# Two graph attention layers in one kernel: where the gather of a layer 0 unit's own rows stands on GpSimd's queue

## The chip, the cores and the metric

The kernel runs on one core of one Trainium2 chip. The metric is the device time of one launch in microseconds. Engines are named as in the profile: PE (TensorE, with PEld for its weight loads), DVE (VectorE), ACT (ScalarE), POOL (GpSimd) and SP (SyncE). POOL and SP issue most of the DMAs; a queue's name with a q (SPq) is its issuing side.

## What is computed

`x` holds 8 graphs of 2048 nodes with 256 channels, `adj` one symmetric adjacency matrix for all of them, in which a node has some 9 neighbours on average. Both layers attend over neighbours, add the input back and normalise:

```python
# layer 0: x = layernorm(x + gnn0(x))
h1, h2, h3 = inp @ W1, inp @ W2, inp @ W3
e = leaky_relu(einsum('bnd,bmd->bnm', h1, h2), 0.2)
e = where(adj > 0, e, -1e12)
h = relu(softmax(e, -1) @ h3)
# layer 1: x = layernorm(x + gnn1(x)), 4 heads of 64
q = (h @ W).reshape(B, N, 4, 64)
e = leaky_relu(e_src[:, :, None] + e_dst[:, None], 0.2)   # q . a_src, q . a_dst
attn = softmax(where(adj > 0, e, -9e15), axis=2)
h = elu(einsum('bijh,bjhd->bihd', attn, q))
```

## The kernel before, in words

**Tiling.** The nodes are sorted by degree and cut into 16 tiles of 128 (`order[:, t]` holds the node numbers of tile `t`). `SLOTS` gives each tile the number K of neighbour slots that its largest node needs: 12 for the sparsest tile to 36 for the densest. A unit is one tile of one half of the batch (4 graphs) in one layer, so there are 64 units: `units` lists 32 of layer 0 (half 0, then half 1, each from the sparsest tile to the densest), then 32 of layer 1. For each slot k of a unit, an indirect DMA on POOL gathers, for 128 nodes, the row of their k-th neighbour: 4 graphs x 256 channels in float32, 4 KB for a node, 512 KB in all. Layer 0 gathers from `xg[h]`, a copy of `x` with the 4 graphs of half h side by side, layer 1 from `qg[h]`.

**A layer 0 unit** goes through four generators.
- `before0` (L525 to L544) gathers the unit's own 128 rows into `xo` (L526, L527; the helper's DMA is L196), and has SP copy them, rearranged, to `xr` for the residual (L531, four DMAs). After four ticks PE transposes `xo` (`transposed`, L417; ACT copies the result, L419), and `projected` (L427) multiplies it by W1 W2^T to give `g`.
- `logits0` multiplies the gathered rows by `g` on DVE (L562: 4 instructions a slot, one a graph) and takes the softmax over the K slots.
- `sums0` makes diagonal matrices of the weights on ACT (`dg`, L659) and adds the weighted rows on PE (L639, 16 matmuls a slot).
- `after0` transposes the sums, multiplies by W3, adds `xr` (L699 on DVE), takes the statistics (L384) and normalises (L395 to L407 on ACT and DVE), writes the rows (L714), and projects them for layer 1 (L723); POOL scatters that to `qg` (L204).

**The ring.** Gathered rows go into a ring of 16 buffers of 2 slots each (`CHUNK`); `chunk_job` issues a chunk's two gathers. A buffer comes free when PE has summed its second slot, so POOL waits at a gather for that matmul. In the first half of layer 0, the ring also takes the adjacency rows (`nb`, L196) from which `neighbours` makes each tile's list on DVE (L505 to L519).

**The order of the work.** The program is written out as a simulation: `tick` (L955) lets `pump` issue all chunk gathers for which there are credits, advances the logits by up to two slots, and each of the queues `starts`, `ends` and `lists` by up to two steps. The main loop (L972) runs through the units; each slot of `sums` is a tick. When half of unit j's slots are summed (L990), `before` of unit j + 3 is put on `starts`, so its first step, with the gather of `xo`, is issued in the next ticks. `before` of the first three units is queued at the start. As unit j = 2 to 9 opens, POOL also issues a part of the copy `xg[1]` (L984), which marks those openings in the trace. POOL's instructions keep exactly the order in which the program issues them; those of the other engines are ordered by the scheduler of the framework, which goes by the program's order and by when it takes their inputs to be ready. Every engine then works through its list in order.

**Buffers.** `xown` has two buffers for `xo`; one comes free when PE's transposes and SP's four copies have read it. `xres` has three for `xr`; one comes free when L699 of its unit has read it, and SP waits for that at L531.

Of the kernel before, what the change touches and what calls it, by code (L numbers as in the profile page):

```python
# [11 lines left out]
F32 = mybir.dt.float32  # L12
# [10 lines left out]
P = 128  # L23
# [106 lines left out]
def fast_path(  # L130
# [26 lines left out]
    NT = N // P  # L157
    KC = C // P
    HB = B // 2
    HC = HB * C  # L160
# [9 lines left out]
    xop = ctx.enter_context(tc.tile_pool(name="xown", bufs=2))  # L170
# [20 lines left out]
    def wide_tile(name):  # L191
        return wp.tile([P, 2 * QW], F32, tag="t", name=name)

    def gather(dst, table, index):

        nc.gpsimd.indirect_dma_start(  # L196
            out=dst, out_offset=None, in_=table, in_offset=AT(ap=index, axis=0),
            bounds_check=table.shape[0] - 1, oob_is_err=False,
        )
# [12 lines left out]
    xg = [tc.dram_tile([N, HC], F32, name=f"xg_{h}") for h in range(2)]  # L212
# [102 lines left out]
    order = const.tile([P, NT], I32, tag="order", name="order")  # L315
# [32 lines left out]
    def checks():  # L348

        worst = wide_tile("worst")[:, :P]  # L350
        nc.gpsimd.memset(worst, 0.0)
        bad = const.tile([P, NT + 3], F32, tag="bad", name="bad")
        found, known = bad[:, NT + 1 : NT + 2], bad[:, NT + 2 : NT + 3]
        nc.vector.tensor_scalar(bad[:, :NT], degs, 0.5, None, ALU.is_lt)
        listless = wide_tile("listless")[:, :total]
        nc.vector.tensor_scalar(listless, neg, 0.0, 0.0, ALU.is_lt, ALU.add, accum_out=found)
        nc.vector.tensor_reduce(known, degs, AX.X, ALU.add)
        nc.vector.tensor_tensor(known, known, found, ALU.add)
        nc.vector.tensor_scalar(bad[:, NT : NT + 1], known, float(total), None, ALU.not_equal)
        nc.vector.tensor_reduce(worst[:, 0:1], bad[:, : NT + 1], AX.X, ALU.max)  # L360
        yield
        pb = ps_tile("ps_bad")
        nc.tensor.transpose(pb[:, :P], worst, ident)
        yield
        most = const.tile([P, 1], F32, tag="most", name="most")
        nc.vector.tensor_reduce(most[0:1, :], pb[0:1, :P], AX.X, ALU.max)
        nc.vector.tensor_copy(flag, most[0:1, :])
        yield
        nc.vector.scalar_tensor_tensor(half, half, 2.0 * N, orderR, ALU.mult, ALU.add)
        for h in range(2):  # L370
            for j in range(2):
                nc.vector.tensor_scalar(
                    oidx[:, h, j], half, float((h * HB + j) * N), None, ALU.add
                )
# [37 lines left out]
    def transposed(src, name, dst):  # L412

        for i in range(2):
            pt = ps_tile(f"ps_t_{name}_{i}")
            for j in range(4):
                nc.tensor.transpose(pt[:, ts(j, P)], src[:, ts(4 * i + j, P)], ident)  # L417
            yield
            nc.scalar.copy(dst[:, ts(i, 512)], pt)  # L419
        yield  # L420

    def projected(srcT, weight, name, evict):
        for i in range(2):
            pp = ps_tile(f"ps_p_{name}_{i}")
            for j in range(2):
                for k in range(KC):
                    nc.tensor.matmul(  # L427
                        pp[:, ts(j, C)],
                        lhsT=srcT[:, ts((2 * i + j) * KC + k, P)],
                        rhs=weight[:, k, :],  # L430
                        start=(k == 0),
                        stop=(k == KC - 1),
                    )
            yield
            evict(i, pp)
        yield

    class Unit:
        def __init__(self, layer, h, t):
            self.layer, self.h, self.t = layer, h, t  # L440
            self.K = SLOTS[t]
            self.name = f"{layer}_{h}_{t}"

            n = self.K if self.K <= RING * CHUNK * 3 // 4 else -(-self.K // 2)
            self.parts = [(k, min(n, self.K - k)) for k in range(0, self.K, n)]
            self.chunks = [[] for _ in self.parts]
            self.p = [None] * len(self.parts)
            self.ps = [None] * len(self.parts)

            self.m, self.s = [], []  # L450
            self.ready = False


# [39 lines left out]
    def neighbours(t):  # L493
        K, o = SLOTS[t], offs[t]
        while t not in loaded:
            yield
        v = loaded[t].bitcast(I16)[:, :N]
        if t in up[:3]:
            numbered(loaded[t])
            nc.vector.memset(loaded[t][:, N // 2 :], 0.0)  # L500


        some = sp.tile([P, 8 * BLOCKS], F32, tag="some", name=f"some_{t}", bufs=2)
        for i in range(BLOCKS):
            nc.vector.max(some[:, ts(i, 8)], v[:, N * i // BLOCKS : N * (i + 1) // BLOCKS])  # L505
            if i % 8 == 7:
                yield
        credits[0] += 1
        rounds = -(-K // 8)
        m = sp.tile([P, 40], F32, tag="m", name=f"m_{t}")  # L510
        for i in range(rounds):
            nc.vector.max(m[:, ts(i, 8)], some)
            if i + 1 < rounds:
                nc.vector.match_replace(some, m[:, ts(i, 8)], some, 0.0)
            yield
        nc.vector.tensor_scalar(neg[:, o : o + K], m[:, :K], 0.5, LOWEST, ALU.is_lt, ALU.mult)
        far = sp.tile([P, 40], F32, tag="far", name=f"far_{t}", bufs=2)[:, :K]
        nc.vector.tensor_scalar(far, m[:, :K], 0.5, FAR, ALU.is_lt, ALU.mult)
        nc.vector.scalar_tensor_tensor(  # L519
            idx[:, o : o + K], m[:, :K], 1.0, far, ALU.subtract, ALU.add  # L520
        )
        listed[t] = True


    def before0(u):  # L525
        xo = xop.tile([P, HC], F32, tag="xo", name=f"xo_{u.name}")  # L526
        gather(xo, xg[u.h][:, :], order[:, u.t : u.t + 1])  # L527
        u.xr = xrp.tile([P, 2, HW], F32, tag="xr", name=f"xr_{u.name}")
        for r in range(2):
            for c in range(2):  # L530
                nc.sync.dma_start(  # L531
                    u.xr[64 * c : 64 * c + 64, r, :], xo[64 * r : 64 * r + 64, ts(c, HW)]
                )
        for _ in range(4):
            yield
        xT = wide_tile(f"xT_{u.name}")
        yield from transposed(xo, f"x_{u.name}", xT)
        while scored[0] < u.index - 1:
            yield
        u.g = gp.tile([P, HC], F32, tag="g", name=f"g_{u.name}")  # L540
        yield from projected(
            xT, w.A, f"g_{u.name}", lambda i, pp: nc.scalar.copy(u.g[:, ts(i, 512)], pp)
        )
        u.ready = True  # L544
# [369 lines left out]
    units = [Unit(0, h, t) for h in range(2) for t in up]  # L914
# [19 lines left out]
    for j, u in enumerate(units):  # L934
        u.index = j
    before = (before0, before1)
    logits = (logits0, logits1)
    sums = (sums0, sums1)
# [8 lines left out]
    def finish(u):  # L947
        yield from after[u.layer](u)
# [6 lines left out]
    def tick(limit):  # L955
        pump()
        while late and late[0][0] <= clock[0]:
            late.popleft()[1]()
        for _ in range(2):
            if ahead[0] < limit:  # L960
                ahead[0] += next(stream, 0)
        for queue in queues:
            for _ in range(min(len(queue), 2)):
                if queue and next(queue[0], queue) is queue:
                    queue.popleft()
        clock[0] += 1
# [5 lines left out]
    for j, u in enumerate(units):  # L972
        begun = False
        if 0 < j and j + 2 < NT:
            lists.append(neighbours(up[j + 2]))
        if j == NT:
            ends.append(checks())
        while len(ends) > 1:
            tick(0)
        if 2 <= j < 10:  # L980
            b, i = divmod(j - 2, 2)
            n = ts(i, N // 2)

            nc.gpsimd.dma_start(xg[1][n, ts(b, C)], x[HB + b, n])  # L984
        left = float(u.K)
        for share in sums[u.layer](u):
            ahead[0] -= share
            left -= share
            tick(left + units[min(j + 1, len(units) - 1)].K + LEAD)
            if not begun and left <= u.K / 2 and j + 3 < len(units):  # L990
                begun = True
                v = units[j + 3]
                starts.append(before[v.layer](v))
        ends.append(finish(u))
# [300 lines left out]
```

## Time and profile before

| | us |
|---|---|
| median of 3 runs | 2709.94 (2703.99 to 2711.37) |
| the profiled execution's own time | 2598.36 |
| its span, first to last instruction | 2596.3 |
| busy: PE, DVE, ACT, POOL | 1816.4 (70%), 2148.3 (83%), 1441.4 (56%), 1532.3 (59%) |
| first and last gather of `xo` | 99.22 and 1417.09 |
| one gather of `xo` on POOL (median of 32) | 1.07 |
| mean granted TensorE clock | 0.85 |

Times in views of the trace are counted from the span's start. A line of the timeline has the start, the duration, the engine and the kernel's line, the operation, output and inputs, and in brackets how long the engine stood idle before it and what ended that. A line of the waits has who waited for what, the sum, the number of times and the longest. Layer 0 fills the profile from about 95 us to 1600 us and layer 1 the rest. The setup before it sorts the nodes.

### The profile page before, as it was taken

The numbers are of one execution on the slowest core, as the hardware profiler recorded it, in microseconds if no ns is written. First come the engines' busy times: TensorE is split into PE (matmuls) and PEld (weight loads), VectorE is DVE, ScalarE is ACT, GpSimd is POOL, SyncE is SP. The second block draws the span as 40 slices with busy tenths as digits, with TensorE's granted clock in tenths as the row PEclk, the third lists the DMA queues.
The fourth block names the chain that finished last, engine by engine and source line by source line (L and its number), as shares of the span: only waits on it lengthen the run. The fifth ranks groups of instructions, "written<-read, shape, count | busy, mean of one in ns | idle before, by whom it ended". The sixth has DMA issues, their size and how long they took to land. (4 is left out here: it accounts for less than half of the span.)

```text
span 2596.3 us, 52231 instructions
## 1 busy us (share of the span) xinstructions
PE 1816.4 (70%) x16675; PEld 989.4 (38%) x16675; DVE 2148.3 (83%) x7073; ACT 1441.4 (56%) x4849; POOL 1532.3 (59%) x1486
## 2 busy tenths in 40 slices
PE   1167797878778787788888878756475666764774
PEld 0145464545445455455555544212121222221221
DVE  6799899899889677777788885789888788988896
ACT  6245475656566556655666657454356556643455
POOL 3464455555555444535455555677677777776774
PEclk9588898989888788988898989878788788887877
DMA  9898787888875566767788768898799999987993
GB/s 382 276 338 273 257 313 267 302 285 280 269 270 194 186 218 240 247 231 235 255 264 284 257 206 273 301 342 327 273 341 355 349 339 367 349 320 270 325 358 106
DMA packets 249419, 734.92 MB, mean 283 GB/s; under 512 B 63200, under 2 KB 72544, under 8 KB 246704
## 3 DMA queue, kind: packets, MB, share of 16 engines
q0 software_dynamic: 192512, 645.89, 70.4%
q1 hardware_dynamic: 55360, 84.44, 9.6%
q8 instruction: 135, 2.21, 0.3%
q14 instruction: 148, 1.21, 0.1%
q10 hardware_dynamic: 1264, 1.18, 0.1%
HBM read 708.35 MB, written 76.09 MB: 302 GB/s over the span
## 5 line engine op out<-in xcount | busy, mean ns | idle before, releaser
L562 DVE CUSTOM_DVE_ANT_0 j<-s,g 128x256 bf16<-128x256 f32 x2384 | 1007.7, 423 | 197.7 <-DMA s<-xg,idx 127.2
L196 POOL DMA_INDIRECT s<-xg,idx x596 | 634.3, 1064 | 625.4 <-PE acc L639 413.5
L639 PE MATMUL acc<-s,ident 64*64 64x512 f32 x4768 | 610.9, 664 | 350.9 <-issue 296.7
L639 PE MATMUL acc<-s,dg 64*64 64x256 f32 x9536 | 706.1, 418 | 187.7 <-ACT dg L659 176.1
L196 POOL DMA_INDIRECT s<-qg,idx x596 | 606.7, 1018 | 242.0 <-issue 130.4
L659 ACT ACTIVATE dg<-twice,e 128x64 f32<-128x64 f32 x2384 | 617.6, 337 | 107.3 <-PE acc L639 101.8
L840 DVE TENSOR_TENSOR s<-s,p 128x2048 f32<-128x2048 f32 (+1 forms) x260 | 574.0, 2229 | 0.0
L639 PEld LDWEIGHTS acc<-s,dg 64*64 64x64 f32 x9536 | 383.1, 144 | 452.1 <-ACT dg L659 256.3
L639 PEld LDWEIGHTS acc<-s,ident 64*64 64x64 f32 x4768 | 210.4, 149 | 743.8 <-issue 600.0
L836 ACT ACTIVATE s<-s,e 128x64 f32<-128x64 f32 x1408 | 342.7, 335 | 47.7 <-DVE e L804 39.6
L395 ACT ACTIVATE z<-st,roots 128x4 f32<-128x4 f32 x64 | 19.1, 298 | 410.1 <-DVE st L384 410.1
L562 DVE DVE_READ_ACCUMULATOR2_ANT e<- 128x1 f32 x2384 | 194.0, 81 | 0.0
L204 POOL DMA_INDIRECT out_dram<-o,oidx x128 | 130.6, 1020 | 68.1 <-ACT o L407 32.2
L774 DVE TENSOR_TENSOR e<-s,own 128x32 f32<-128x32 f32 (+1 forms) x306 | 55.7, 186 | 121.5 <-DMA s<-qg,idx 120.3
L417 PE MATMUL ps_t_x<-ident,xo 128*128 128x128 f32 x256 | 55.4, 359 | 120.0 <-DMA xo<-xg,order 120.0
L723 PE MATMUL ps_q<-wqs,x1T 128*128 128x264 f32 x512 | 137.8, 407 | 2.1 <-ACT x1T L419 2.1
L427 PE MATMUL ps_p_h<-w_sb,hT 128*128 128x256 f32 x512 | 130.4, 399 | 5.6 <-ACT hT L419 5.6
L427 PE MATMUL ps_p_g<-A,xT 128*128 128x256 f32 x512 | 131.9, 404 | 1.8 <-ACT xT L419 1.5
L427 PEld LDWEIGHTS ps_p_g<-A,xT 128*128 128x128 f32 x512 | 98.0, 199 | 32.0 <-issue 8.1
L427 PEld LDWEIGHTS ps_p_h<-w_sb,hT 128*128 128x128 f32 x512 | 94.4, 194 | 40.8 <-issue 13.2
L723 PEld LDWEIGHTS ps_q<-wqs,x1T 128*128 128x128 f32 x512 | 98.3, 199 | 29.6 <-issue 7.7
L407 ACT ACTIVATE o<-xr,nmr,rstd 128x256 f32<-128x256 f32 x128 | 66.5, 589 | 76.1 <-DVE nmr L403 67.7
(138 smaller groups left out, 1467.9 us busy)
## 6 DMA issues: line engine op xcount, KB each, us to landing
adj<-in_adj_dram SPq DMA_DIRECT2D x16, 1024.0 KB
xr<-xo SPq DMA_DIRECT2D x128, 128.0 KB
x1s<-y SPq DMA_DIRECT2D x32, 512.0 KB
xr<-x1s SPq DMA_DIRECT2D x32, 512.0 KB
s<-xg,idx POOLq DMA_INDIRECT x596
s<-qg,idx POOLq DMA_INDIRECT x596
edges<-adj SPq DMA_DIRECT2D x16, 512.0 KB
xg<-in_x_dram SPq DMA_DIRECT2D x4, 2048.0 KB
```

Source lines behind the costliest of these rows:

```text
L196: nc.gpsimd.indirect_dma_start(out=dst, out_offset=None, in_=table, in_offset=AT(ap=index, axis=0), bounds_check=table.shape[0] - 1, oob_i ...
L204: ins = nc.gpsimd.indirect_dma_start(out=table, out_offset=AT(ap=index, axis=0), in_=src, in_offset=None)
L407: nc.scalar.activation(dst[:, b, :], y[:, b, :], AF.Identity, bias=nmr[:, b : b + 1], scale=rstd[:, b : b + 1],)
L417: nc.tensor.transpose(pt[:, ts(j, P)], src[:, ts(4 * i + j, P)], ident)
L427: nc.tensor.matmul(pp[:, ts(j, C)], lhsT=srcT[:, ts((2 * i + j) * KC + k, P)], rhs=weight[:, k, :], start=(k == 0), stop=(k == KC - 1),)
L562: nc.vector.tensor_tensor_reduce(out=jt, in0=rows[:, s, ts(b, C)], in1=u.g[:, ts(b, C)], scale=1.0, scalar=0.0, op0=ALU.mult, op1=ALU.add, ...
L639: nc.tensor.matmul(out, lhsT=lhsT, rhs=rhs, start=(k == 0 and j == 0), stop=(k == K - 1 and (j == 1 or diag is None)), tile_position=(64 * ...
L659: nc.scalar.activation(diag[:, b, :], twice, AF.Copy, scale=u.p[i][:, b, k : k + 1])
L723: nc.tensor.matmul(pq[:, : C + 2 * H], lhsT=x1T[:, ts(i * KC + k, P)], rhs=w.sqs[:, k, j * H : j * H + CD + H], start=(k == 0), stop=(k == ...
L774: nc.vector.tensor_tensor(e[:, c * CHUNK : c * CHUNK + ns, :].rearrange("p s (b g) -> p s b g", b=HB), rows[:, :ns, :].rearrange("p s (b w ...
L836: nc.scalar.activation(v[:, a, g, :], v[:, a, g, :], AF.Copy, scale=pv[:, a, g : g + 1])
L840: nc.vector.tensor_tensor(v, v, pv.unsqueeze(3).to_broadcast([P, n * HB, H, D]), ALU.mult)
```

## The change

The two lines that allocate `xo` and issue its gather move from `before0` to a function of their own, `own_rows`. It is called as unit j opens, for unit j + 3, as long as that is a unit of layer 0 (NT is 16). `before0` finds the rows already gathered, and issues the gather itself only for the first three units. The rest of `before0`, with SP's copies and PE's transposes, still starts in the middle of unit j. No instruction is added or taken away.

```diff
@@ class Unit
             self.m, self.s = [], []
+            self.xo = None
             self.ready = False
@@
+    def own_rows(u):
+        u.xo = xop.tile([P, HC], F32, tag="xo", name=f"xo_{u.name}")
+        gather(u.xo, xg[u.h][:, :], order[:, u.t : u.t + 1])
+
     def before0(u):
-        xo = xop.tile([P, HC], F32, tag="xo", name=f"xo_{u.name}")
-        gather(xo, xg[u.h][:, :], order[:, u.t : u.t + 1])
+        if u.xo is None:
+            own_rows(u)
+        xo = u.xo
         u.xr = xrp.tile([P, 2, HW], F32, tag="xr", name=f"xr_{u.name}")
@@ the main loop, as unit j opens
             nc.gpsimd.dma_start(xg[1][n, ts(b, C)], x[HB + b, n])
+        if j + 3 < 2 * NT:
+
+            own_rows(units[j + 3])
         left = float(u.K)
         for share in sums[u.layer](u):
```

For j = 0 the call stands ahead of the first tick, so u3's gather becomes the first thing that POOL issues for layer 0.

## The prediction

> **What bounds the kernel now.** Units of layer 0 are called u0 to u31 in the order in which they run (u0 to u15 batch half 0, u16 to u31 half 1); uj "opens" where its sums begin. I began with the busy shares on the page (DVE 83%, PE 70%, the largest two), then asked for the waits of each engine by stage, because layer 0 has two regimes and the change touches only layer 0. (The page's chain of waits holds only the kernel's tail here, 0% of the span, and carries nothing.) The waits of the second stretch, 660 to 1430 us, from four answers (us in total, times, longest):
>
> ```profile
> PE ps_t_x L417 <- DMA xo<-xg,order: 74.6, 16, 7.8
> PE acc L639 <- ACT dg L659: 66.3, 28, 6.8
> DVE j L562 <- DMA s<-xg,idx: 110.4, 83, 6.7
> ACT z L395 <- DVE st L384: 90.6, 16, 10.5
> POOL s L196 <- PE acc L639: 299.6, 90, 15.0
> ```
>
> PE's largest wait is for the gather that the change moves, about once per unit. POOL mostly waits for PE to give back a ring buffer, and DVE for the chunks that POOL then gathers. So it is one loop: PE frees, POOL gathers, DVE scores, ACT makes diagonals, PE sums. In the first stretch the same two waits are nearly absent, and the table by stage says why (us of the window, then busy us of PE, PEld, DVE, ACT, POOL, then clock, DMA share, GB/s):
>
> ```profile
> PE ps_t_x L417 <- DMA xo<-xg,order: 0.5, 1, 0.5
> 200.00:660.00 460.00, 372.78 (x3720) 246.24 (x3720) 418.17 (x2065) 279.74 (x963) 247.53 (x235) 0.89 0.83 284
> 660.00:1430.00 770.00, 620.11 (x6105) 399.05 (x6109) 599.33 (x2750) 463.07 (x1595) 378.41 (x358) 0.88 0.72 240
> ```
>
> Up to 660 us DVE is busy 418 of 460 us (91%): it also builds neighbour lists and sets the pace. After it DVE is busy 78% and PE 81%; neither is full and each waits for the other through the ring. DMA is at 0.72, so bandwidth does not decide. One stall in the timeline (start, us, engine and line, [idle before]):
>
> ```profile
> 1096.41 1.21 POOL L196 DMA_INDIRECT xo<-xg,order  x1 [0.31 <-issue]
> ...
> 1109.36 0.99 POOL L196 DMA_INDIRECT s<-xg,idx  x1 [6.24 <-PE acc L639]
> ...
> 1122.11 1.00 POOL L196 DMA_INDIRECT s<-xg,idx  x1 [7.22 <-PE acc L639]
> 1105.25 1.09 PE L417 MATMUL ps_t_x<-ident,xo 128*128 128x128 f32 x4 [7.13 <-DMA xo<-xg,order]
> 1106.13 1.06 PE L417 MATMUL ps_t_x<-ident,y 128*128 128x128 f32 x4
> 1107.12 1.92 PE L639 MATMUL acc<-s,dg 64*64 64x256 f32 x16
> 1108.98 0.66 PE L417 MATMUL ps_t_x<-ident,xo 128*128 128x128 f32 x4
> 1106.52 0.43 DVE L562 CUSTOM_DVE_ANT_0 j<-s,g 128x256 bf16<-128x256 f32 x1 [2.85 <-DMA s<-xg,idx]
> ...
> 1126.80 0.43 DVE L562 CUSTOM_DVE_ANT_0 j<-s,g 128x256 bf16<-128x256 f32 x1 [5.23 <-DMA s<-xg,idx]
> ```
>
> The gather issued at 1096.41 has landed at 1105.25. PE stood 7.13 us, POOL 6.24 us behind it for a ring buffer, and DVE 2.85 us behind POOL; 1126.80 is the same chain again after POOL's 7.22 us.
>
> **The change, part by part.**
>
> *The gather leaves the middle.* The transposes keep their place (four ticks into `before0`, which still starts at half a unit). The mean time from the end of the gather's issue to the first transpose is 7.1 us in the 16 stalls. Counting the chunk gathers on POOL (596 in the trace, 596 in the program) gives the new place: right after the last chunk that the previous unit's buffers allow. For u18 to u27 that is where POOL stood 3.5 to 10.1 us; for u22 it is 1114.89, before the row 1122.11, and u25's gather was issued at 1141.38, so it moves 26.5 us ahead (21 to 26.5 in these ten). 21 is three times 7.1, so all 16 waits end: 74.6 us of PE.
>
> *The clock behind a stall.* The four transposes at 1105.25 take 1.09 us, those at 1108.98 take 0.66. The same sequence without a stall, from the first stretch:
>
> ```profile
> 494.66 0.66 PE L417 MATMUL ps_t_x<-ident,xo 128*128 128x128 f32 x4
> ```
>
> From the first four to the second four it is 2.0 us there (the second are at 496.70) and 3.7 us here: 1.7 us lost, in 15 of the 16 stalls (after the shortest, 1.95 us, the four take 0.63). That would be another 25 us. The Trainium skill (TensorE: Matmul & The Clock Gate, Part 1) puts the loss of clock after an idle window of about 3.4 us. By it, the 11 stalls above 3.4 us would pay (19 us); by the rows those of 2.7 to 3.3 us do too. The rows decide.
>
> *What of it reaches the end.* Freed PE time moves the end only while DVE also has waits to give up, since behind PE the next late thing is DVE (its logits, and its statistics, for which ACT holds the diagonals: the `z` row). I took, for u15 to u31's 17 intervals between two such gathers, the smaller of PE's xo wait and DVE's wait for chunks: the sum is 66 us; with 1.7 us of clock per stall it is 86. In the unit shown, 7.13 beside 2.85 + 5.23: both POOL waits start from PE and would end earlier by the stall, so DVE can follow. A gather's own 7 us stay, so some of DVE's waits will too. I take 66 and leave the clock out as what is lost there. Ends: 29, if only DVE's waits in the 12 us after the old place end (29.0 by count), and 86.
>
> *The gather arrives at the opening.* Its 1.0 to 1.2 us on POOL (+0.3 between issues) fall into POOL's idle 3.5 to 10.1 us in the second stretch: nothing. If that gap were gone they'd cost 1.4 us a unit. Its 512 KB take 2.2 us at the stage's 240 GB/s, and are through before the chunks behind the gap. In the first stretch the opening is seen by `xg<-in_x_dram` (L984), which is issued there:
>
> ```profile
> 503.76 0.99 POOL L196 DMA_INDIRECT s<-xg,idx  x1 [0.30 <-issue]
> 504.76 0.84 POOL L984 DMA_DIRECT2D xg<-in_x_dram  x1
> 505.90 1.03 POOL L196 DMA_INDIRECT s<-xg,idx  x1 [0.30 <-issue]
> ```
>
> Here it stands inside a burst: up to 12 units x 1.4 = 17 us, if DVE has nothing in hand; nothing if it has. DVE waited for chunks only 12.0 us in this stretch, so I take 4.
>
> *The first issue.* u3's gather now precedes the three neighbour loads that start everything (first at 95.28): 1.3 us on POOL, and its 512 KB ahead of theirs, 1.9 us at the 276 GB/s of the page's second slice, largely the same time. POOL then issues without a pause from 113 to 170, and there 1.5 us (the old place, 170.49) go. I take +1.4; ends 0 and 3.2.
>
> *Buffers and queues.* `xown` has two. At uj's opening u(j+2)'s rows hold one; the other is free once u(j+1)'s four copies to `xr` on SP have read it. For u22 they are issued at 1088.34 to 1090.8, the gather at 1114.9: 24 us to spare. The least I find is u3 (copies of u4 end at 241.9, opening 248.84: about 5). While u3's early rows hold one buffer, u0, u1 and u2 share the other; their gathers at 134.55 and 155.05 come after the copies of u0 (110.9) and u1 (about 144). So no new wait: 0. If there were one, every chunk gather and scatter on POOL would queue behind it. SP and its order don't change.
>
> *A rule against it.* The Trainium skill (DMA: Bandwidth & Descriptors, Anatomy of one DMA) prices a transfer from GpSimd at 2.0 us plus bytes/436e3, 3.2 us for these 512 KB. By that, only 18 us of the 74.6 would be due to the gather's place (each gather's issue end + 3.2, less PE's arrival). The trace has 7.1 us, since chunk gathers stand ahead of it in the queue. The trace decides.
>
> Sum: 66 - 4 - 1.4 = 60 us. The profiled execution (2598.36 us, span 2596.3) would become about 2538. The timed runs are 4% longer (2703.99 to 2711.37), where, the profile cannot say; I take the same 60 us off their median: 2709.94 - 60 = 2650.
>
> **The rivals.**
>
> *Only half follows.* PE's freed time returns as `acc <- ACT dg` because DVE keeps its pace. For it: ACT stood 90.6 us for DVE's statistics, PE 66.3 behind diagonals. Against: DVE itself stands 110.4 us. The gain is 29 - 5 = 24: 2686.
>
> *It doesn't do what it says.* The new place still lies behind a blocked ring gather, so rows land as late as before. Against: the count puts it ahead of the wait. About 2710.
>
> *Slower: the buffer.* If the gather at the opening is given the buffer of u(j+2), POOL stands until that unit's copies: for u22 those of u24 (1133.96 + 2.5, landing about 1138), 23 us, of which 7 are idle anyway. 16 us a unit in which no chunk is gathered; POOL has 299.6/17 = 17.6 us a unit of waiting to make it up with, so between 0 and 16; at half, 29 units x 8 = +232: about 2942. It decides where u(j+1)'s copies land after the opening: more than 24 us later than now in u22, 5 in u3. Against: those margins.
>
> **How the numbers follow.** First case 0.60 (own range 2624 to 2672, from 86 to about 38); only half 0.22 (2672 to 2704); no effect 0.09; buffer 0.09. A measurement of this kernel can tell about 0.3%, 8 us, from no change. Faster: 0.59 + 0.20 = 0.79; same 0.12; slower 0.09. The range 2624 to 2704 leaves out the last two cases.
>
> **What would show it.** Right: PE's row for `xo<-xg` near 0 after 200 us; the four transposes at 0.66; POOL's `xo` gather in its gap after an opening; DVE's 110 us down by 50 to 70; layer 1 starting some 60 us earlier, with its own length unchanged. Only half: `acc <- ACT dg` up by some 40 and DVE's row down by under 35. Slower: a POOL row `xo L196 <- DMA xr<-xo` of many us. I'd be wrong above all if the transposes moved ahead with the gather, or PE's order in layer 0 changed otherwise.

## The result and the profile after

The changed kernel takes 2662.56 us (median of 6 runs, 2658.91 to 2669.87) where the kernel before, run again beside it, takes 2707.18 (6 runs, 2693.03 to 2711.37). The ratio is 0.9848, 95% interval 0.9828 to 0.9869: 44.6 us less. 60 us less had been forecast. Its profiled execution took 2664.78 us, with a span of 2662.9.

One thing has to be known before any two traces are compared: chips differ for this program. The kernel before takes about 2594 us on some (group A here) and 2702 to 2721 on others (group B). Which group a run belongs to is told by its times; what makes the difference was not found. The profile of before that is shown above is of group A, that of after is of group B. So the comparisons below are made within a group, and the kernel before was traced again in both.

The waits of the changed kernel (group B) in the second stretch, 660 to 1430 us (who waits for what, us in total, times, longest):

```profile
POOL s L196 <- PE acc L645: 240.4, 114, 13.8
ACT z L395 <- DVE st L384: 52.2, 10, 8.7
DVE j L568 <- DMA s<-xg,idx: 48.3, 39, 7.3
PE acc L645 <- ACT dg L665: 28.3, 12, 6.7
```

PE's row for `xo<-xg`, its largest before, is not there at all. (Lines are five or six further down than in the kernel before: L562 is now L568, L639 is L645.) In the table by stage, with the columns of before (us, busy us of PE, PEld, DVE, ACT, POOL, clock, DMA share, GB/s), PE is now as busy in the second stretch as in the first (86 and 85%) and DVE nearly (84 and 88%):

```profile
200.00:660.00 460.00, 389.15 (x3618) 248.12 (x3617) 405.59 (x1998) 272.18 (x931) 234.87 (x223) 0.90 0.80 273
660.00:1430.00 770.00, 663.47 (x6562) 420.45 (x6561) 647.32 (x2971) 484.66 (x1688) 411.37 (x390) 0.93 0.77 259
```

The kernel before, in the same group and the same 770 us:

```profile
660.00:1430.00 770.00, 632.02 (x6146) 402.58 (x6149) 601.28 (x2758) 461.90 (x1579) 375.40 (x361) 0.90 0.73 241
```

DVE does 2971 instructions instead of 2758, POOL 390 instead of 361. In the first stretch there is no such step: DVE does 1998 instructions there, and did 2029 before.

One opening in POOL's timeline of the changed kernel:

```profile
1122.20 1.09 POOL L196 DMA_INDIRECT s<-xg,idx  x1 [0.30 <-DVE e L568]
1123.60 1.11 POOL L196 DMA_INDIRECT xo<-xg,order  x1 [0.30 <-issue]
1129.50 0.99 POOL L196 DMA_INDIRECT s<-xg,idx  x1 [4.79 <-PE acc L645]
```

The gather of own rows is the last thing POOL issues before it stands 4.79 us for a ring buffer, so its 1.11 us and the issue gap are taken from a wait. PE, at a place where transposes stand:

```profile
1113.69 0.70 PE L645 MATMUL acc<-s,dg 64*64 64x256 f32 x6 [0.75 <-issue]
1114.33 0.66 PE L417 MATMUL ps_t_x<-ident,xo 128*128 128x128 f32 x4
1114.82 0.60 PE L417 MATMUL ps_t_x<-ident,y 128*128 128x128 f32 x4
1115.35 1.09 PE L645 MATMUL acc<-s,dg 64*64 64x256 f32 x16
1116.37 0.66 PE L417 MATMUL ps_t_x<-ident,xo 128*128 128x128 f32 x4
```

No idle time stands ahead of the four transposes, they take 0.66 us instead of 1.09, and the 16 sums between the two groups of four take 1.09 instead of 1.92. Here the loss behind a stall is gone with the stall. (In the second stretch 14 of the 17 units' first four take at most 0.67; the other three take 1.11 without a stall ahead of them.)

Where layer 0 gained is read from the last line that SP issues for it, the write of u31's rows. Before, group B, and then the changed kernel:

```profile
734.40 0.33 SPq L714 DMA_DIRECT2D x1s<-y  x1
...
1643.99 0.32 SPq L714 DMA_DIRECT2D x1s<-y  x1
```

```profile
742.84 0.33 SPq L720 DMA_DIRECT2D x1s<-y  x1
...
1598.03 0.32 SPq L720 DMA_DIRECT2D x1s<-y  x1
```

The upper line of each is u12's. The changed kernel is 8.4 us late at u12 and 46.0 us early at u31, so u13 to u31 gain 54.4. The rest, from u31's write to the end of the span, is 2704.8 - 1644.0 = 1060.8 us before and 2662.9 - 1598.0 = 1064.9 after, the same within 4 us. This is the marker for all experiments below: u12's write closes the first stretch, u31's the second.

### The profile page after: what moved, and what is told of

It is laid out like the page before. It is cut to its first block, busy times and chain, and to the rows that moved or that the text cites. A ratio compares the mean times of both kernels' runs of the same rounds, so it can differ in the third digit from the quotient of the medians.

```text
span 2662.9 us, 52259 instructions
## 1 busy us (share of the span) xinstructions
PE 2078.2 (78%) x16675; PEld 1105.1 (42%) x16675; DVE 2154.7 (81%) x7073; ACT 1445.4 (54%) x4849; POOL 1526.7 (57%) x1486
## 4 chain that ended last, share of the span: by engine, by line
DVE 28%; PE 24%; issue 22%; DMA 12%; POOL 7%; ACT 4%; another core or an unknown queue 1%; POOLq 0%; DVEq 0%; ACTq 0%
PE acc L645 19%; DVE j L568 15%; DMA s<-xg,idx 6%; DMA s<-qg,idx 5%; POOL s L196 5%; DVE s L846 4%; ACT s L842 2%; DVE e L568 1%; PE ps_p_h L427 1%; DVE st L384 1%; PE ps_p_g L427 1%; DVE some L506 1%; PE ps_q L729 1%; DVE y L705 1%
## 5 line engine op out<-in xcount | busy, mean ns | idle before, releaser
L568 DVE CUSTOM_DVE_ANT_0 j<-s,g 128x256 bf16<-128x256 f32 x2384 | 1009.0, 423 | 165.7 <-DMA s<-xg,idx 71.2
L645 PE MATMUL acc<-s,ident 64*64 64x512 f32 x4768 | 837.3, 678 | 216.6 <-issue 186.3
L645 PE MATMUL acc<-s,dg 64*64 64x256 f32 x9536 | 750.4, 417 | 174.0 <-ACT dg L665 84.1
L645 PEld LDWEIGHTS acc<-s,ident 64*64 64x64 f32 x4768 | 318.9, 150 | 726.6 <-issue 659.4
L645 PEld LDWEIGHTS acc<-s,dg 64*64 64x64 f32 x9536 | 400.6, 143 | 467.6 <-issue 179.2
L780 DVE TENSOR_TENSOR e<-s,own 128x32 f32<-128x32 f32 (+1 forms) x306 | 56.8, 188 | 193.9 <-DMA s<-qg,idx 150.7
L568 DVE DVE_READ_ACCUMULATOR2_ANT e<- 128x1 f32 x2384 | 194.4, 82 | 0.0
L204 POOL DMA_INDIRECT out_dram<-o,oidx x128 | 128.1, 1001 | 66.3 <-issue 31.7
L427 PEld LDWEIGHTS ps_p_h<-w_sb,hT 128*128 128x128 f32 x512 | 94.3, 194 | 40.6 <-issue 13.6
L796 ACT ACTIVATE e<-e 128x288 f32<-128x288 f32 (+11 forms) x34 | 14.8, 435 | 167.8 <-DVE e L795 129.9
```

What stands on the lines that cost most here:

```text
L204: ins = nc.gpsimd.indirect_dma_start(out=table, out_offset=AT(ap=index, axis=0), in_=src, in_offset=None)
L427: nc.tensor.matmul(pp[:, ts(j, C)], lhsT=srcT[:, ts((2 * i + j) * KC + k, P)], rhs=weight[:, k, :], start=(k == 0), stop=(k == KC - 1),)
L568: nc.vector.tensor_tensor_reduce(out=jt, in0=rows[:, s, ts(b, C)], in1=u.g[:, ts(b, C)], scale=1.0, scalar=0.0, op0=ALU.mult, op1=ALU.add, ...
L645: nc.tensor.matmul(out, lhsT=lhsT, rhs=rhs, start=(k == 0 and j == 0), stop=(k == K - 1 and (j == 1 or diag is None)), tile_position=(64 * ...
L780: nc.vector.tensor_tensor(e[:, c * CHUNK : c * CHUNK + ns, :].rearrange("p s (b g) -> p s b g", b=HB), rows[:, :ns, :].rearrange("p s (b w ...
```

## The experiments

Two theories were set against each other. The first is the prediction's: PE stood for the own rows, POOL behind PE, DVE behind POOL; without PE's stall DVE's waits end too. The second: what counts is the place of the gather on POOL's queue, ahead of or behind chunk gathers, or the gain comes from another part of layer 0. A third question came up with the first traces: what costs more than forecast in the first stretch.

### The kernel before once more (group A, and later group B)

> The kernel before, unchanged, for a trace at the pace of its timed runs: the profiled execution shown so far took 2598 us, the timed runs of the same kernel 2693 to 2711, and the changed kernel's profile 2663. If the first profile was an unusually quick execution, this one takes about 2700 us, the extra 100 us lies mostly in layer 1 (1145 us in the changed kernel's trace against 1056), and layer 0 still shows about 75 us of PE's wait for xo between 660 and 1430 us. If the earlier profile was ordinary, it takes about 2600 again and the two traces can be compared as they are.

Group A: 2600.99 us in the profiled run, median 2593.61 over 18 runs. Its waits from 660 to 1430 us:

```profile
PE ps_t_x L417 <- DMA xo<-xg,order: 73.8, 16, 7.0
PE acc L639 <- ACT dg L659: 66.4, 31, 6.2
DVE j L562 <- DMA s<-xg,idx: 107.4, 84, 7.3
```

These are the rows that the prediction read (74.6, 66.3, 110.4), so they are steady from run to run on group A. u12's write is at 717.66 and u31's at 1622.99.

> The kernel before, for a trace on a chip where it takes about 2710 us, if this job gets one. There the changed kernel's trace has short stops of all engines that name no releaser, layer 1 takes 1065 us instead of 970, and the change gains 41 to 45 us instead of 51. Theory A (the chip stretches everything, the same waits go): layer 1 takes about 1065 us here too, PE's wait for xo is about 75 us again, and the end of layer 0 lies 40 to 60 us behind the changed kernel's. Theory B (the waits for xo are shorter on such a chip, so that less goes): the sum is 60 us or less. On the other kind of chip: about 2600, as the first repetition.

Group B: 2706.92 us, median 2701.82 over 11 runs. Here the same wait is smaller (660 to 1480 us, since the stretch lasts longer):

```profile
PE ps_t_x L417 <- DMA xo<-xg,order: 53.5, 14, 5.8
PE acc L639 <- ACT dg L659: 47.1, 17, 6.8
DVE j L562 <- DMA s<-xg,idx: 101.6, 63, 7.6
```

So on the group that was timed there were 53.5 us of PE's stall to take away, not 74.6.

### The changed kernel again (group A)

> The changed kernel itself, for a trace and times on the chip where the kernel before takes about 2594 us. Theory A (the gain is the wait of PE for xo and what hung on it, and the pace of the chip only stretches both kernels): 0.976 to 0.980 of before, as with the two variants that keep the early gather in the second half of layer 0 (0.9777 and 0.9768), so about 2537. Theory B (the first stretch and the head cost 7 us, as the variant with the early gather only there showed with 1.0022): about 2543, 0.9805. The first result, 0.985, was from a chip where the kernel before takes 2707.

2543.25 us beside 2593.85, ratio 0.9813 (0.9791 to 0.9835): 50.6 us less. u12's write is 4.4 us later than before, u31's 59.5 us earlier (1563.53), so u13 to u31 gain 63.8. A trace is one execution: this one (2534.57) is 8.7 us below the median of its kernel and that of before 7.4 above, so the two traces are further apart than the times. No wait of PE for own rows is left, and DVE's for chunks is (660 to 1430 us):

```profile
DVE j L568 <- DMA s<-xg,idx: 45.5, 41, 7.5
```

### Only the units from the opening of u12 on

```diff
-        if j + 3 < 2 * NT:
+        if 12 <= j and j + 3 < 2 * NT:
```

> The early gather only from u12's opening on, for u15 to u31, where the trace of before has the 74.6 us of PE's wait. Theory A (the gain is those waits, and the first stretch and the head give back about 5 us): 5 us less than the changed kernel, about 2657. Theory B (the first stretch gives back 15 to 25 us through its burst and its head): about 2640. Rival C (the gain has another source, such as a changed order of the other engines): half of the gain or less, 2685 or more.

Group A: 2536.09 us, ratio 0.9768 (0.9750 to 0.9786): 57.5 us less by the medians (55.5 to 64.8 by the interval), more than the whole change gives there. The waits from 660 to 1430 us, to be set beside those of before in group A:

```profile
PE acc L645 <- ACT dg L665: 81.5, 35, 6.7
DVE j L568 <- DMA s<-xg,idx: 48.4, 41, 7.3
POOL s L196 <- PE acc L645: 254.9, 108, 15.6
```

73.8 us of PE's stall end; 15.1 come back as a longer wait for diagonals; DVE's chunk wait falls by 59.0. u12's write is at 716.75 (0.9 earlier than before), u31's at 1559.48 (63.5 earlier): the gain lies from u12 on.

A changed order of the other engines is not behind it. Compared instruction by instruction with the kernel before, PE goes through the same 687 steps (a step is a run of matmuls of one kind) in the same order, and only at four places do transposes come 4 to 10 matmuls earlier. Some 20 of ACT's 4849 instructions and some 30 of DVE's 7073 stand elsewhere.

> The early gather only from u12's opening on, once more beside the kernel before. It was 0.9768 on a chip with 2594 us. If the slower chip's smaller gain comes from the first stretch and the head, it is 0.977 to 0.979 there as well; if the second stretch itself gives less on such a chip, 0.983 or above.

The same kernel in group B: 2649.58 us, ratio 0.9801 (0.9773 to 0.9829): 52.2 us less. That falls between the two expectations, so the time alone does not decide. u12's write is 0.3 us and u31's 56.8 us earlier than before, so u13 to u31 gain 56.5. DVE's chunk wait falls from 101.6 to 51.7 us (660 to 1480 us).

### Only the openings of u0 to u11

```diff
-        if j + 3 < 2 * NT:
+        if j < 12:
```

> The complement: the early gather only at the openings of u0 to u11, for u3 to u14. There the trace of before has next to no wait for xo after 200 us. Theory A: about 5 us slower than before. Theory B: 15 to 25 us slower than before. Rival C: faster than before by 15 us or more.

Group A: 2600.81 us, ratio 1.0022 (1.0010 to 1.0033), 7.2 us more by the medians (2.6 to 8.6 by the interval), where there was nothing to end. With the run before it this is 7.2 - 57.5 = -50.3, beside -50.6 of the whole change. Within the intervals the two halves add up, and the first one costs; that they agree to 0.3 is chance.

The trace shows how far the markers can be trusted. u12's write is 4.7 us later than before, but u31's is 3.8 earlier, so u13 to u31 gain 8.5 us although PE's wait for own rows is all there (73.6 us). A gain between the two markers is known to some 8 us, no better.

### The gather left in the middle, the transposes later

In the kernel before, `before0` goes nine ticks on instead of four between the gather and the transposes. The gather keeps its old place on POOL's queue.

```diff
-        for _ in range(4):
+        for _ in range(9):
```

> The kernel before with the gather left in the middle, but with nine ticks instead of four between it and the transposes of xo, so that PE comes five slots (about 5 us or more) later to them. Theory A (what counts is only that PE does not stand at the transposes; the place of the gather on POOL's queue is worth little): most of the waits end, since their mean is 4.7 us, and the time is 0.980 of before, about 2540. Rival D (half of the gain comes from the gather having left the burst in the middle and moved into POOL's gap): 0.988, about 2563. Rival E (g comes later and DVE waits for it): 1.00 or above.

Group A: 2550.28 us, ratio 0.9834 (0.9813 to 0.9855). The waits from 690 to 1560 us:

```profile
PE acc L639 <- ACT dg L659: 103.5, 50, 9.8
DVE j L562 <- DMA s<-xg,idx: 39.9, 31, 3.3
```

The same window of the kernel before (group A), for comparison:

```profile
DVE j L562 <- DMA s<-xg,idx: 112.3, 88, 7.3
PE acc L639 <- ACT dg L659: 87.3, 38, 9.9
PE ps_t_x L417 <- DMA xo<-xg,order: 70.9, 15, 7.0
```

PE's stall is gone without the gather having moved, and DVE's chunk wait falls by 72.4. u12's write is 12.3 us later than before (729.99 against 717.66), u31's 50.7 earlier (1572.26): from u12 on the gain is 63.1, that of the second half alone (62.6) within what the markers can tell. So in the second stretch the end of PE's standing is enough for the whole gain, and nothing is left that the gather's place on POOL's queue would have to explain. What this version loses, it loses in the first stretch, where it too had no stall to end.

### The gather after a quarter of the unit

```diff
+            if j + 3 < 2 * NT and left <= 0.75 * u.K and units[j + 3].xo is None:
+                own_rows(units[j + 3])
```

This stands in the loop over `sums`, in place of the call at the opening.

> The early gather after a quarter of unit j's slots instead of at its opening: some 10 us ahead of the middle, where the gather needs 7.1 us to land. Theory A: the waits for xo end as with the change, 0.977 of before, about 2535, and the first unit and the bursts of the first stretch are left alone. If the gap on POOL after the opening is what makes the gather free (rival D): 0.983, about 2550.

Group A: 2536.55 us, ratio 0.9790 (0.9766 to 0.9813), on the same chip as the changed kernel (0.9813, 0.9791 to 0.9835): not told apart by time. In the trace no `xo` wait is left on PE in the second stretch; u12's write is 7.9 us earlier than before instead of 4.4 later, u31's 62.1 earlier, against 59.5. So 54.2 of its gain lie behind u12, and 7.9 ahead of it, where no stall was to end; where those come from was not looked into.

### All openings but the first

```diff
-        if j + 3 < 2 * NT:
+        if 0 < j and j + 3 < 2 * NT:
```

> The change, but not for the first unit: u3's rows are gathered in the middle of u0 as before. The changed kernel's trace has u2's transposes 13 us later than the trace of before. Theory A (the early gather costs 1.4 us at the head, the rest of the 13 us is not from the change): within 3 us of the changed kernel, about 2660. Theory B (the early gather, which holds one of the two buffers until u3's copies and stands ahead of the neighbour loads, costs the 13 us): about 2650.

Group A: 2534.84 us, ratio 0.9777 (0.9763 to 0.9791), 58.8 us less. u12's write stands where it stood before (717.67), u31's is 64.0 us earlier. So the calls for u4 to u14 cost nothing by u12 as long as u3's is not made, and the same bursts of POOL in the first stretch are there.

### u3's gather one tick later

As above, with the first call moved behind the neighbour loads and u0's own rows:

```diff
+            if j == 0 and units[3].xo is None:
+                own_rows(units[3])
```

> The change, but u3's rows are gathered one tick later, behind the three neighbour loads and u0's own rows instead of ahead of them. In the changed kernel the first neighbour row is worked on at 104.3 us instead of 101.1, and u0 is written 2 us later; without the call for the first unit the time was 0.9777 of before, with it 0.9813. Theory A (the head's loss is the delay of the neighbour loads by the 512 KB ahead of them): u0 is written at 208 us as before, and the time is 0.978. Theory B (the loss comes from u3's rows holding one of the two buffers, or from the order that the scheduler makes of it): 0.981.

Group B: 2680.33 us beside 2721.23, ratio 0.9849 (0.9826 to 0.9873), the changed kernel's own ratio. u0's rows are now written 1.6 us earlier than in the group B trace of before, so the delay at the head is gone, and u12's are still 11.8 us later. (That trace is of another chip, on which the kernel before is 0.7% faster, so the 11.8 are rough.) The delay of the neighbour loads is not what costs.

### Only the first opening

```diff
-        if j + 3 < 2 * NT:
+        if j == 0:
```

> The kernel before with the call made at one opening only: as u0 opens, for u3 (the gather of u3's rows ahead of the neighbour loads). All other gathers stay in the middle. Theory A (the loss of the first stretch comes from this one call, for u1 to u11's calls cost nothing there: the runs without the first call and with the second half alone differ by 1 us): 6 to 9 us slower than before, ratio 1.0022 to 1.0035, and the rows of u8 written some 5 us later than before. Theory B (the loss is spread over the twelve calls, each standing in a burst of POOL): no more than the 1.4 us of the prediction's head, at most 3.2, ratio 1.000 to 1.0012.

Group B: 2703.09 us beside 2702.64, ratio 1.0001 (0.9987 to 1.0016). u0's write is 2.9 us later, u2's 2.9 us earlier and u12's 0.4 us earlier than before (group B). No cost of the call alone shows that lasts; up to 4 us would lie within the interval. I had expected it to carry the loss (6 to 9 us); that fell.

### One buffer for the own rows

The version without the first call, with the pool cut from two buffers to one, so that a gather must wait until the last unit's rows have been read:

```diff
-    xop = ctx.enter_context(tc.tile_pool(name="xown", bufs=2))
+    xop = ctx.enter_context(tc.tile_pool(name="xown", bufs=1))
```

> The change without the first unit, and with one buffer for xo instead of two. POOL's order of work is the same, but at u(j)'s opening the buffer is still held by u(j+2)'s rows, so POOL must stand there until SP has copied them, a few us ahead of the middle, with all chunk gathers behind it. This makes the case that I held for the slower one. By the working of the prediction it costs 16 us in each of 28 units less what POOL can make up, 0 to 448 us, at half 224: about 2760 where the kernel with two buffers takes 2535. If the chunks in the ring cover the wait, under 2560.

Group B: 3045.12 us, ratio 1.1191 (1.1161 to 1.1221). The wait that the prediction named as the sign of its slower rival, over the whole trace:

```profile
POOL xo L196 <- DMA xr<-xo: 614.1, 27, 30.0
```

614.1/27 is 22.7 us for each, and the time is 365 us over the 2680.33 of the version with u3's gather one tick later, on the same chip, 13 us for each of 28 units. (PE stands 72.4 us for own rows in this run too, so not all of the 365 need be POOL's wait.) In the two traces of the change no such wait of POOL was found.

## Why the prediction was right, and where its size was off

**The chain held.** Every sign that was named came: the `xo` row of PE is gone after 200 us, the four transposes take 0.66 (in group A in 16 of 17 units), the gather stands in POOL's gap behind an opening (in 11 of the 17 units in group B, ahead of a wait of 1.8 us or more), DVE's chunk wait fell by 53 (group B, 660 to 1480 us: 101.6 to 48.3) to 62 us (group A, 660 to 1430 us: 107.4 to 45.5), and layer 1 starts 46 (B) to 59 us (A) earlier at a length that stayed within 7 us. PE's order stayed, which the prediction named as what would prove it wrong above all: besides the four places named above, the change orders it otherwise only at u3's transposes, at about 180 us. The run with later transposes shows more than the change itself could: the end of PE's standing is enough, wherever the gather lies.

**The term of 66.** In group A, from whose profile it was worked out, it measured 62.6 (second half alone), 63.1 (transposes later) and 63.8 (whole change) between the markers, and 57.5 by the times of the second half alone. In group B, whose times were to be forecast, it measured 54.4 (whole change) and 56.5 (second half alone). The step that failed is "where, the profile cannot say; I take the same 60": the timed chips were not only 4% longer, they also had less of the wait to give, 53.5 us where the profile had 74.6. The prediction's own sum, taken once more from the group B trace of before, gives 53 us where it gave 66. The same program so gains less where PE's stall is smaller, which speaks for the stall as the cause. This is 66 - 54.4 = 11.6 of the 15.4 us that are missing, as exactly as the markers tell. Why PE waits less for these rows in group B is not known.

The rule of the smaller wait was hardly tried, though: in 14 of the 17 intervals PE's wait was the smaller, so that the sum is little else than PE's wait.

**The clock.** The 25 us behind the stalls were left out "as what is lost" in the coupling. The clock did rise, as these rows of the second stretch in group A show (before, then after):

```profile
660.00:1430.00 770.00, 618.43 (x6114) 398.23 (x6115) 601.89 (x2763) 464.19 (x1598) 383.75 (x361) 0.89 0.72 241
660.00:1430.00 770.00, 644.62 (x6703) 411.28 (x6705) 657.66 (x3019) 489.48 (x1730) 417.31 (x392) 0.93 0.78 263
```

The loop turned some of PE's time into waits for diagonals (+15.1 in the second half alone). The two together left what the chunk waits allowed, as the step had it; that they cancel so nearly was not worked out, and is luck as far as this record goes. The 25 itself was rough: the 1.7 us was read off one stall, while between the first four and the second four transposes lie 2.1 to 4.7 us in the 16 stalls. Nor does the length of a stall alone decide: in the group B trace of before the four transposes take 0.63 after a wait of 3.72 us, and 1.09 after one of 2.03.

**The DMA share.** "DMA is at 0.72, so bandwidth does not decide" is an average. Around the stall that the prediction shows (1098 to 1105 us) the DMA engines of the kernel before are full:

```profile
1090.00:1107.00 17.00, 8.82 (x88) 4.84 (x88) 10.41 (x52) 10.48 (x38) 10.38 (x10) 0.85 1.01 353
```

So the own rows were called for in the middle of a burst of chunk gathers, which fits the 7.1 us that they took. What such a gather takes outside a burst was not measured.

**The terms of 4 and 1.4.** They measured 4.4 (A) and 8.4 (B) in the traces at u12, and 7.2 (2.6 to 8.6) timed by the run of the first half alone, against 5.4. The sum is near, but its parts are not confirmed. The calls for u4 to u14 alone cost nothing by u12 (717.67, before 717.66), and u3's alone shows no cost (1.0001). In these traces only both together make the stretch longer. The head's 1.4 is seen, as 1.2 to 2.9 us at u0's write, but u2 no longer shows it where u3's call stands alone. What the two do together isn't settled. A row that grows in the first stretch is POOL's wait for a list of neighbours to be made on DVE, which frees the ring's buffers (200 to 690 us, group A; before and then the changed kernel):

```profile
POOL s L196 <- DVE some L505: 44.3, 9, 9.8
DVE j L562 <- DMA s<-xg,idx: 16.7, 19, 1.9
```

```profile
POOL s L196 <- DVE some L506: 68.9, 9, 12.9
DVE j L568 <- DMA s<-xg,idx: 22.4, 22, 4.4
```

But it is 55.4 us, and DVE's row 22.6, in the run without the first call, which lost nothing; so these rows go along with the loss and do not decide it. Two causes remain possible. One is that u3's rows hold one of the two buffers while u4's want the other; no wait of POOL for that buffer is in the traces. The other is that the scheduler orders the other engines' work differently. The traces lean to it: of the versions with early gathers, the three that lose here (the whole change, the first half alone, u3's gather one tick later) have DVE's and ACT's instructions in one and the same order up to 690 us, and each of the three that lose nothing (all but the first, only the first, a quarter in) has another one. That this order is the cause was not tried.

**The rivals.** "Only half follows" asked for +40 on `acc <- ACT dg` and under 35 off DVE's row. In group A the first is +15.1 and the second 59.0 for the second half alone; in group B the first even falls, from 47.1 to 40.6. It fell. "It doesn't do what it says" fell with PE's row. "The buffer" did not occur, and its price was well judged: 22.7 us held instead of 23, and 13 us for a unit, inside the 0 to 16 that were given, above the half that was taken. The margins were read rightly, and the second buffer is what the change stands on.

**A better version.** Leaving the first calls out keeps the whole of the second stretch: 57.5 to 58.8 us less in group A (0.9768 and 0.9777) and 52.2 in group B (0.9801, 0.9773 to 0.9829), where the whole change gives 50.6 and 44.6.

A slip in the text ahead of the prediction: a node has some 17 neighbours, itself among them, not 9. No step used it.

## What to carry to other kernels

When an engine of a closed loop stands for a transfer, add up its waits unit by unit, and take the next engine's wait where that is smaller. Here this came within 4 us of what the traces showed, in both groups, though mostly because the stalled engine's own wait was the smaller. In a stretch without such a stall the same edit brings nothing and may cost. A load may be issued early, at the opening of a unit or a quarter into it, only as far as a second buffer is surely free; moving the consumer a few steps later ends the same stall. Before a sum from a trace is set against a time, make sure that both are from chips that run the program alike, or trace the kernel again where it is timed.

## What was not expected of the hardware

The two groups of chips. On group B layer 1 takes 1060 to 1072 us in the traces with two buffers, on group A 969 to 976, all with the same program for that layer. A window inside layer 1 of the kernel before, in group A and then in group B:

```profile
1700.00:2500.00 800.00, 492.37 (x3888) 167.36 (x3884) 686.78 (x920) 399.91 (x1387) 596.21 (x583) 0.82 0.90 330
```

```profile
1720.00:2600.00 880.00, 696.33 (x3929) 266.91 (x3932) 692.49 (x923) 407.49 (x1396) 591.70 (x586) 0.84 0.85 301
```

DVE, ACT and POOL have nearly the same busy time for nearly the same work, which takes 880 us instead of 800. The granted clock is no lower (0.84 and 0.82), but the transfers run at 301 GB/s instead of 330, and a matmul record is longer on the average (696.33/3929 is 177 ns, 492.37/3888 is 127). In group B POOL also stands for something that the trace can't name (the kernel before, 1660 to 2662 us):

```profile
POOL s L196 <- remote: 84.6, 47, 2.5
PE acc L639 <- remote: 21.2, 4, 10.8
```

In group A POOL has no such row in the same part. What these stops are was not tested and stays open.
